# Twelve projections of an attention layer by seven products of half-size blocks in place of eight

## The chip, the cores and the metric

The kernel runs on one core of a Trainium2 chip. The metric is the device time of one execution in microseconds (us), the median of repeated runs. The core has a matrix engine (TensorE, "PE" in the profile; its weight loads are "PEld"), which multiplies into a memory of its own called PSUM (in banks; a tile of 128 x 512 float32 numbers fills one), and three engines that work on vectors: VectorE ("DVE"), ScalarE ("ACT") and GpSimd ("POOL"). SyncE ("SP") issues transfers. GpSimd is given operands in ordinary on-chip memory alone in this kernel; what lies in PSUM is taken out by VectorE or ScalarE. Engines run side by side and wait for each other by semaphores.

## The reference, cut to what matters

A batch of 4 images with 512 channels of 32 x 32 = 1024 tokens goes through four layers, each added to its input after a group normalisation. The change touches layer 2 alone, an attention with 8 heads of 64 channels:

```python
def _L2_conv_ref(x, Wq, bq, Wkv, bkv, Wp, bp):
    ...
    q = _conv1x1(x, Wq, bq)                  # 512 x 512 weight on 512 x 1024 values
    kv = _conv1x1(x, Wkv, bkv)
    k, v = jnp.split(kv, 2, axis=1)
    ...
    attn = jnp.einsum('bhct,bhcs->bhts', q, k) * SCALE
    attn = jax.nn.softmax(attn, axis=-1)
    out = jnp.einsum('bhts,bhcs->bhct', attn, v)
    ...
    out = _conv1x1(out, Wp, bp)
    return out

    # --- layer 2 (conv_preact) ---
    x = x + _L2_conv_ref(_gn(x), L2_conv_Wq, ...)
```

Per image that is four projections (q, k, v and the output p), each a product of a 512 x 512 weight and 512 x 1024 values, and between them the scores, the softmax and the weighted sum of v. Everything is in float32. Layer 0 is another attention, layer 1 a gate, layer 3 a search for the 8 nearest of 2048 stored items.

## The kernel before: layer 2

P is 128, NB 512, T 1024 (tokens), C 512, KC 4 (groups of 128 channels), TC 8 (groups of 128 tokens). A projection is 32 matmuls of 128 x 128 weights on 512 columns. Four at a time add up in one bank, and eight fill a tile of two banks, which one operation takes out. The tiles come from a pool of three ("sc"), so the next eight matmuls have another tile:

```python
def project(w, rhs, m, at, evacuate, name="proj"):
    ps = place(at, f"{name}_{m}")            # ps_s.tile([P, 2, NB], F32, tag="sc")
    for n in range(T // NB):
        for k in range(KC):
            pin(nc.tensor.matmul(                            # L197
                ps[:, n, :], w[:, k, m * P:(m + 1) * P], rhs(k, n),
                start=(k == 0), stop=(k == KC - 1)))
    evacuate(flat2(ps))
```

`project_tokens` (L209) does the same for v, with tokens as rows. q is taken out by DVE (L935, with bias and the factor SCALE), k by ACT (L942), v by DVE with its bias (L951). The attention of an image is cut into 16 units of four groups of keys; the scores of one unit stand beside the weighted sum of the unit before it:

```python
def scores2(b, u, before=None):
    ...
    nc.scalar.activation(e, scs[len(es)], AF.Exp)            # L967
    ...
    pin(nc.tensor.matmul(sc[:, r, :], I["k"][...], I["q"][...], ...))   # L973
    ...
    # the sum of the exponentials: pairs on GpSimd, pairs of pairs on VectorE
    nc.gpsimd.tensor_add(I["es", m, n], es[0], es[1])        # L987
    nc.gpsimd.tensor_add(two, es[i], es[i + 1])              # L991
    nc.vector.tensor_add(I["es", m, n], I["es", m, n], two)  # L992

def finish2(b):                                              # a head pair's end
    ...                                                      # rs: matmuls with ones, L1027
    nc.scalar.copy(ri, rsp)                                  # L1032
    nc.vector.reciprocal(ri, ri)                             # L1033
    nc.vector.tensor_mul(I["o"][...], pv, ri)                # L1034
    ...                                                      # two small transfers by GpSimd, L1037

def put_out2(b):                                             # output projection and residual
    def add_out(m, ps):
        for n in range(T // NB):
            xr = apool.tile([P, NB], F32, tag="xr", bufs=2, ...)
            nc.sync.dma_start(out=xr, in_=x1[b][:, m, n * NB:(n + 1) * NB])    # L1048
            nc.scalar.activation(xr, xr, AF.Identity, bias=I["tb"]..., scale=s1...)  # L1049
            nc.vector.tensor_add(xr, ps[:, n * NB:(n + 1) * NB], xr)           # L1051
            nc.sync.dma_start(out=x2[b][:, m, n * NB:(n + 1) * NB], in_=xr)    # L1052
            nc.vector.bn_stats(st[:, n, :], xr)                                # L1053
    for m in range(KC):
        project(I["Wp"], tokens(I["o"]), m, None, lambda ps: add_out(m, ps), ...)
```

The loop over the images, cut:

```python
for b in range(B):
    for s, u in enumerate(UNITS2):                  # 16 units
        if s == 5 and not last: load2(b + 1)        # Wq, Wk, Wv of the next image
        if s >= 1: scores2(b, u, UNITS2[s - 1])
        for _ in range(2):
            if s >= 3: next(behind, None)           # small steps of other layers
            if s >= 8: next(ahead, None)            # the next image's normalisation
    if not last:
        for m in range(KC): take_q2(b + 1, m)       # q of the next image
        img[b]["Wp"] = load_w("Wp", ...)
    apply2(b, UNITS2[-1])                           # the last unit's weighted sum
    if not last:
        for m in range(KC): take_k2(b + 1, m)       # k of the next image
    finish2(b)
    if not last:
        for i in range(TC // 2): take_v2(b + 1, i)  # v of the next image
        scores2(b + 1, UNITS2[0])                   # its first unit
    put_out2(b)                                     # p of this image
```

The sums and the last head pair's end thus fall into the time of q and of v; the last DVE and POOL operations of the attention are still under way when q begins. Image 0's q, k and v are made in layer 1's part, outside this loop.

Of the kernel before, what the change touches and what calls it, by code (L numbers as in the profile page):

```python
# [41 lines left out]
def fast_net(ctx: ExitStack, tc: tile.TileContext, a: dict, out: bass.AP, flag: bass.AP):  # L42
# [33 lines left out]
    bp2 = chan(a["bp"], "bp2")  # L76
    fcb = chan(a["fc_b"], "fcb")
# [818 lines left out]

    count = [0]
# [33 lines left out]
    def take_q2(b, m, at=None):  # L931
        I = img[b]
        if m == 0:
            I["q"] = big("q", f"q2_{b}")
        project(I["Wq"], tokens(I["xn"]), m, at, lambda ps: pin(nc.vector.tensor_scalar(  # L935
            I["q"][:, m, :], ps, bq2[:, m:m + 1], SCALE, ALU.add, ALU.mult)), f"q2_{b}")
# [8 lines left out]
    def take_v2(b, i, at=None):  # L945
        I = img[b]
        if i == 0:
# [3 lines left out]
            lambda ps: pin(nc.vector.tensor_add(  # L951
                I["v"][:, 2 * i:2 * i + 2, :], ps,
                bv2.rearrange("p c -> p () c").to_broadcast([P, 2, C]))), f"v2_{b}")

    def scores2(b, u, before=None):
# [8 lines left out]
        def exp2():  # L964
            e = places2[:, count[0] % 6]
            count[0] += 1
            nc.scalar.activation(e, scs[len(es)], AF.Exp)  # L967
# [17 lines left out]
        if t0 == 0:  # L985
            I["es", m, n] = sums2[:, (2 * m + n) % 2]
            nc.gpsimd.tensor_add(I["es", m, n], es[0], es[1])  # L987
            es = es[2:]
        for i in range(0, len(es), 2):
            two = pair_sum[:, (t0 + i) // 2 % 2]  # L990
            nc.gpsimd.tensor_add(two, es[i], es[i + 1])  # L991
            nc.vector.tensor_add(I["es", m, n], I["es", m, n], two)  # L992
# [45 lines left out]

    def put_out2(b):
        I = img[b]  # L1040
        s1 = l2[b][1]
        mv = small.tile([P, KC, 2], F32, tag="mv", name=f"mv_d{b}")

        def add_out(m, ps):
            st = small.tile([P, 2, 6], F32, tag="bnst", name=f"st_d{b}_{m}")
            for n in range(T // NB):
                xr = apool.tile([P, NB], F32, tag="xr", bufs=2, name=f"xr_c{b}_{m}_{n}")
                nc.sync.dma_start(out=xr, in_=x1[b][:, m, n * NB:(n + 1) * NB])  # L1048
                nc.scalar.activation(  # L1049
                    xr, xr, AF.Identity, bias=I["tb"][:, m:m + 1], scale=s1[:, m:m + 1])  # L1050
                nc.vector.tensor_add(xr, ps[:, n * NB:(n + 1) * NB], xr)  # L1051
                nc.sync.dma_start(out=x2[b][:, m, n * NB:(n + 1) * NB], in_=xr)  # L1052
                nc.vector.bn_stats(st[:, n, :], xr)  # L1053
# [1027 lines left out]
```

## Time and profile before

| what | value |
|---|---|
| median of 3 runs | 2745.2 us (2741.17 to 2746.28) |
| span of the profiled run | 2741.6 us |
| mean TensorE clock granted | 0.98 of full speed |
| layer 2 in the span | about 1375 to 2225 us |
| attention stages of image 0, 1, 2, 3 | 1375 to 1508, 1628 to 1746, 1865 to 1985, 2104 to 2225 us |
| projection stages between them | 1508 to 1628, 1746 to 1865, 1985 to 2104 us |

The span is the time from the first to the last instruction of one execution; it is read in windows, stage by stage, since each stage has a limit of its own. For each window the profile gives the busy time of each engine with the number of its instructions, and the clock that TensorE was granted. The rows of groups give, for a line of the kernel and an engine, what is written from what, the shape, how often, the busy time and the mean of one in ns, and then the idle time of the engine ahead of them with what ended it. A group with DVE as its engine that reads a tile written by PE takes a result out of PSUM. Three such rows of layer 2, which the steps below speak of:

```profile
L1032 ACT COPY ri_c<-rs_c 128x512 f32<-128x512 f32 x32 | 18.7, 585 | 49.9 <-PE rs_c L1027 49.9
L1051 DVE TENSOR_TENSOR xr_c<-p,xr_c 128x512 f32<-128x512 f32 x24 | 15.5, 687 | 42.3 <-PE p L197 38.2 <-ACT xr_c L1049 4.1
L650 DVE SCALAR_TENSOR_TENSOR xr<-mx,bproj,xr 128x512 f32<-128x512 f32 x6 | 4.5, 745 | 11.4 <-PE mx L197 8.9 <-DMA xr<-in_x 2.5
```

### The profile page before, as it was taken

Reading aid. Unit: us, or ns where it says so; the run is one execution under the profiler, and the core shown is the slowest. Engines: PE = TensorE matmul, PEld = TensorE weight load, DVE = VectorE, ACT = ScalarE, POOL = GpSimd, SP = SyncE. Lnnn points to the kernel's source line nnn. Section 1 sums busy time; section 2 is a strip of 40 time slices with the busy share of each in tenths; the row PEclk is TensorE's granted clock in tenths of the full one; section 3 lists DMA queues with packets and bytes.
Section 4 is the critical chain, followed back from the end, with each engine's and each line's share of the span. In section 5 each row is a group of like instructions: output and inputs, shape, how many; then the busy total and the mean of one; then the engine's idle time right before and its main releaser. Section 6 shows DMA issues by size and latency. Waiting matters only on the chain.

```text
span 2741.6 us, 46996 instructions
## 1 busy us (share of the span) xinstructions
PE 2593.0 (95%) x18286; PEld 1180.3 (43%) x18286; DVE 1522.8 (56%) x2386; ACT 1007.6 (37%) x1149; POOL 1266.2 (46%) x1955
## 2 busy tenths in 40 slices
PE   8988999989989898989999999999999999999995
PEld 3443544545445444545433433343343334444442
DVE  5487337871588526873235224513623537788886
ACT  0565336551565426552154025214502622121210
POOL 2266325552455514653067017305702735666664
PEclk9999999999999999999999999999999999999997
DMA  2577438880687627785310030021002016767665
GB/s 78 128 206 204 128 93 219 218 216 28 172 216 202 164 69 193 205 207 199 116 32 1 31 123 1 16 77 62 1 31 92 1 48 189 220 186 216 185 183 148
DMA packets 159321, 349.82 MB, mean 128 GB/s; under 512 B 32361, under 2 KB 65129, under 8 KB 155378
## 3 DMA queue, kind: packets, MB, share of 16 engines
q1 hardware_dynamic: 86304, 167.04, 21.2%
q0 software_dynamic: 51200, 142.93, 19.3%
q10 hardware_dynamic: 21586, 36.76, 4.6%
q8 instruction: 147, 2.41, 0.4%
q14 instruction: 84, 0.69, 0.1%
HBM read 178.57 MB, written 33.69 MB: 77 GB/s over the span
## 4 chain that ended last, share of the span: by engine, by line
PE 82%; DMA 7%; ACT 4%; DVE 2%; issue 1%; POOL 1%; SPq 1%; ACTq 0%; POOLq 0%; DVEq 0%
PE at L1094 16%; PE sc_c L973 7%; PE pv_c L1006 7%; PE sc L451 7%; PE mx L197 7%; PE pv L511 6%; PE pt L410 4%; DMA s<-ss 4%; PE p L197 4%; PE sc L197 4%; PE v L209 3%; PE k L197 3%; PE q L197 3%; PE pt L684 3%; ACT ss L457 2%; PE mx L471 2%
## 5 line engine op out<-in xcount | busy, mean ns | idle before, releaser
L484 DVE STREAM_TRANSPOSE eT<-e 128x1024 f32<-128x1024 f32 x256 | 317.6, 1242 | 273.9 <-ACT e L478 272.0
L464 POOL DMA_DIRECT2D s<-ss x512 | 259.8, 515 | 384.4 <-ACT ss L457 299.6
L1111 POOL DMA_INDIRECT got<-in_mem,ix x256 | 280.2, 1095 | 208.3 <-DVE tmx L1117 92.3
L457 ACT COPY ss<-sc 128x1024 f32<-128x1024 f32 x256 | 258.9, 1011 | 264.4 <-PE sc L451 212.7
L967 ACT ACTIVATE eT<-sc_c 128x1024 f32<-128x1024 f32 x256 | 247.9, 1021 | 275.3 <-PE sc_c L973 213.3
L500 DVE BATCH_NORM_STATS2 st<-e 128x6 f32<-128x256 f32 x1024 | 341.6, 406 | 0.0
L451 PE MATMUL sc<-k,q 64*32 64x512 f32 x4096 | 287.1, 617 | 22.5 <-ACT ss L457 17.6
L991 POOL TENSOR_TENSOR e<-eT 128x1024 f32<-128x1024 f32 x96 | 231.3, 2412 | 164.7 <-ACT eT L967 133.2
L478 ACT ACTIVATE e<-mx 128x1024 f32<-128x1024 f32 x256 | 262.5, 1029 | 65.5 <-PE mx L471 28.0
L992 DVE TENSOR_TENSOR eT<-eT,e 128x1024 f32<-128x1024 f32 x96 | 132.8, 1384 | 274.0 <-POOL e L991 274.0
L511 PE MATMUL pv<-eT,v 128*64 128x128 f32 x4096 | 256.5, 279 | 0.0
L973 PE MATMUL sc_c<-q,k 64*128 64x512 f32 x1024 | 243.2, 614 | 11.3 <-ACT eT L967 9.0
L511 PEld LDWEIGHTS pv<-eT,v 128*64 128x64 f32 x4096 | 226.1, 139 | 63.9 <-issue 62.3
L1006 PE MATMUL pv_c<-eT,v 128*64 128x512 f32 x1024 | 234.4, 600 | 0.0
L471 PE MATMUL mx<-s,wmix 32*32 32x512 f32 x4096 | 159.6, 625 | 45.0 <-DMA s<-ss 44.9
L1135 DVE SCALAR_TENSOR_TENSOR acc<-got,et,acc 128x512 f32<-128x512 f32 x224 | 168.4, 752 | 8.0
L1033 DVE RECIPROCAL ri_c<-ri_c 128x512 f32<-128x512 f32 x32 | 107.0, 3345 | 96.1 <-ACT ri_c L1032 96.1
L973 PEld LDWEIGHTS sc_c<-q,k 64*128 64x128 f32 x1024 | 94.9, 189 | 144.0 <-issue 74.7
L1099 ACT COPY att<-at 128x1024 f32<-128x1024 f32 x64 | 64.8, 1012 | 217.8 <-PE at L1094 217.6
L987 POOL TENSOR_TENSOR eT<-eT 128x1024 f32<-128x1024 f32 x32 | 76.0, 2374 | 147.0 <-ACT eT L967 146.8
L587 POOL TENSOR_TENSOR o<-pv,rb 64x256 f32<-64x256 f32 x128 | 111.1, 868 | 67.1 <-ACT pv L574 60.2
L1006 PEld LDWEIGHTS pv_c<-eT,v 128*64 128x64 f32 x1024 | 70.9, 138 | 155.2 <-issue 154.6
(317 smaller groups left out, 3325.5 us busy)
## 6 DMA issues: line engine op xcount, KB each, us to landing
s<-ss SPq DMA_DIRECT2D x512, 128.0 KB
s<-ss POOLq DMA_DIRECT2D x512, 128.0 KB, 4.4
rb<-r POOLq DMA_DIRECT2D x64, 128.0 KB, 5.9
o<-o SPq DMA_DIRECT2D x32, 256.0 KB
xr<-in_x ACTq DMA_DIRECT2D x32, 256.0 KB
x<-xr SPq DMA_DIRECT2D x32, 256.0 KB
xr_c<-x SPq DMA_DIRECT2D x32, 256.0 KB
x<-xr_c SPq DMA_DIRECT2D x32, 256.0 KB
```

What stands on the lines that cost most here:

```text
L197: pin(nc.tensor.matmul(ps[:, n, :], w[:, k, m * P:(m + 1) * P], rhs(k, n), start=(k == 0), stop=(k == KC - 1),))
L451: pin(nc.tensor.matmul(sc[m * NS:(m + 1) * NS, r, :], q[r * HD:(r + 1) * HD, m, s * NS:(s + 1) * NS], k_[r * HD:(r + 1) * HD, m, n * NB:(n ...
L457: pin(nc.scalar.copy(ss[:, :, n * NB:(n + 1) * NB], sc))
L464: pin(relays[r].dma_start(out=s2[r * KC + m::NH], in_=ss[m * NS:(m + 1) * NS, r, :]))
L478: pin(nc.scalar.activation(e[:, half].rearrange("p r qq k -> p (r qq k)"), flat2(pairs[f"mx{half}"]), AF.Exp))
L484: pin(nc.vector.transpose(eT[:, j % 2].rearrange("p b (qq i r) x -> p i r qq b x", qq=2, i=4)[:, i, 2 * half:2 * half + 2], e[:, half].rea ...
L500: pin(nc.vector.bn_stats(st[:, i, 2 * half + r, qq, :], e[:, half, r, qq, :]))
L511: pin(nc.tensor.matmul(pv[r * HD:(r + 1) * HD, gp, :], I["v"][:, t, g * HD:(g + 1) * HD], eT[:, j % 2, t, :, 4 * g:4 * g + 4], start=(t == ...
L973: pin(nc.tensor.matmul(sc[:, r, :], I["k"][r * HD:(r + 1) * HD, m, t * P:(t + 1) * P], I["q"][r * HD:(r + 1) * HD, m, n * NB:(n + 1) * NB] ...
L1006: pin(nc.tensor.matmul(pv[r * HD:(r + 1) * HD, :], I["v"][:, t, h * HD:(h + 1) * HD], e[:, r, :], start=(t == 0), stop=(t == TC - 1),))
L1094: pin(nc.tensor.matmul(sc[:, n * NB:(n + 1) * NB], xn3[b][:, k, tt * P:(tt + 1) * P], memT[k][:, i0:i0 + NB], start=(k == 0), stop=(k == K ...
L1111: pin(nc.gpsimd.indirect_dma_start(out=got[:, i, :], out_offset=None, in_=a["mem"], in_offset=bass.IndirectOffsetOnAxis(ap=ix[:, i:i + 1], ...
```

## The change

A product of two matrices, each cut into 2 x 2 blocks, takes eight products of blocks. Strassen's scheme in Winograd's form takes seven, at the price of sums of blocks: four sums on the weight's side, four on the values' side, and seven on the products' side. The change does this for twelve of layer 2's sixteen projections: q, k and v of images 1 to 3 and p of images 0 to 2. The sums of weight blocks are made by GpSimd, those of value blocks by VectorE, both ahead of the projection; those of products by VectorE as the products come. It comes in two halves a projection, each with two tiles of the pool of three. The whole list of what it alters:

- `seven_w`, `seven_x`: the sums ahead of use. `seven`: the order of the seven products and what takes them out.
- The factor SCALE moves from q to the exponential, since bias and factor would not fit q's new evacuation.
- The bias of v is left out of v and carried: the softmax's weights add to one, so bv goes through to the output as Wp times bv, a column that `carry_bias` makes once and that is added to the output's bias.
- The eight pieces of the image that p's output is added to are loaded ahead of p, six of them into a region that the stored items of layer 3 held until now; those items are loaded in the last image.
- The sums of the last unit's exponentials are written behind q (`later`), the next image's normalisation begins two units earlier, and the statistics of a piece are taken two pieces later.

The core of the diff, with cuts:

```diff
+    def seven_w(w, nm):
+        ...
+        nc.gpsimd.tensor_add(s1, block(1, 0), block(1, 1))
+        nc.gpsimd.tensor_sub(s2_, s1, block(0, 0))
+        nc.gpsimd.tensor_sub(s4, block(0, 1), s2_)
+        nc.gpsimd.tensor_sub(block(1, 0), block(0, 0), block(1, 0))
+        return None, block(0, 0), block(0, 1), s4, block(1, 1), s1, s2_, block(1, 0)
+    def seven_x(x, places):
+        ...
+        nc.vector.tensor_sub(t1, block(0, 1), block(0, 0))
+        nc.vector.tensor_sub(block(0, 1), block(1, 1), block(0, 1))
+        nc.vector.tensor_sub(t2, block(1, 1), t1)
+        nc.vector.tensor_sub(t4, block(1, 0), t2)
+        return None, block(0, 0), block(1, 0), block(1, 1), t4, t1, t2, block(0, 1)
+    def seven(product, put, nm):
+        ag = ps_s.tile([P, 2, NB], F32, tag="sc", name=f"ag_{nm}")
+        de = ps_s.tile([P, 2, NB], F32, tag="sc", name=f"de_{nm}")
+        product(1, ag[:, 0], True)
+        u2 = apool.tile([P, NB], F32, tag="o1", name=f"u2_{nm}")
+        nc.scalar.copy(u2, ag[:, 0])
+        product(6, ag[:, 1], True)
+        nc.vector.tensor_add(u2, u2, ag[:, 1])
+        product(7, de[:, 1], True)
+        u3 = apool.tile([P, NB], F32, tag="o2", name=f"u3_{nm}")
+        nc.vector.tensor_add(u3, u2, de[:, 1])
+        product(5, de[:, 0], True)
+        put(1, 1, u3, de[:, 0])
+        product(2, ag[:, 0], False)      # adds to p1, still in the bank
+        put(0, 0, None, ag[:, 0])
+        product(4, de[:, 1], False)      # adds to p7
+        put(1, 0, u2, de[:, 1])
+        product(3, de[:, 0], False)      # adds to p5
+        put(0, 1, u2, de[:, 0])
+    def project7(A, X, out, bias, nm):   # q and k; project7_tokens is the same for v
+        for m in range(2):
+            def put(i, j, u, ps):
+                ...
+                if u is None:
+                    nc.scalar.activation(o, ps, AF.Identity, bias=bias[:, c:c + 1])
+                else:
+                    nc.vector.scalar_tensor_tensor(o, u, bias[:, c:c + 1], ps, ALU.add, ALU.add)
+            seven(seven_by_channels(A, X, m), put, f"{nm}_{m}")
...
-            nc.scalar.activation(e, scs[len(es)], AF.Exp)
+            nc.scalar.activation(e, scs[len(es)], AF.Exp, scale=SCALE)
...
+    def carry_bias(b):
+        for m in range(KC):
+            for k in range(KC):
+                pin(nc.tensor.matmul(
+                    ps[:, m:m + 1], img[b]["Wp"][:, k, m * P:(m + 1) * P], bv2[:, k:k + 1], ...))
...
+        def add_block(m, n, u, ps):      # p: one piece of the output
+            xr = I.pop(("xr2", m, n))
+            if u is None:
+                nc.vector.tensor_add(xr, ps, xr)
+            else:
+                y = apool.tile([P, NB], F32, tag="rb", bufs=2, ...)
+                nc.vector.tensor_add(y, u, ps)
+                nc.gpsimd.tensor_add(xr, xr, y)
+            store(m, n, xr)
+            ...                          # ACT scales the piece three further on
...
+            if s in (8, 9) and not last:
+                img[b + 1]["A", key] = seven_w(img[b + 1][key], ...)      # Wq, Wk
...
+            if s == 12 and not last:
+                run_out(ahead)
+                img[b + 1]["X"] = seven_x(img[b + 1]["xn"], thirds(halves2))
         if not last:
-            for m in range(KC):
-                take_q2(b + 1, m)
-            img[b]["Wp"] = load_w("Wp", f"Wp2_{b}")
+            take7(b + 1, "Wq")
+            for add_up in later:
+                add_up()
+            J["A", "Wv"] = seven_w(J["Wv"], f"Wv{b + 1}")
+            I["Wp"] = load_w("Wp", f"Wp2_{b}")
         apply2(b, UNITS2[-1])
         if not last:
-            for m in range(KC):
-                take_k2(b + 1, m)
+            take7(b + 1, "Wk")
+            if b == 0:
+                carry_bias(b)
+            I["A", "Wp"] = seven_w(I["Wp"], f"Wp{b}")
         finish2(b)
...
+            I["O"] = seven_x(I["o"], [...])
+            take7(b + 1, "Wv")
+            nc.gpsimd.tensor_add(I["tb"], I["tb"], cb)
+            for at in range(len(ORDER2)):
+                load_piece2(b, at)
             scores2(b + 1, UNITS2[0])
         put_out2(b)
```

The last image keeps the plain output projection, and image 0 its plain q, k and v.

## The prediction

> **What bounds the kernel now.** I read the page's first part, then the waits of TensorE in layer 2, which the change is confined to (1375 to 2225 us of the span).
>
> ```profile
> PE 2593.0 (95%) x18286; PEld 1180.3 (43%) x18286; DVE 1522.8 (56%) x2386; ACT 1007.6 (37%) x1149; POOL 1266.2 (46%) x1955
> ```
>
> ```profile
> PE sc_c L973 <- ACT eT L967: 9.0, 4, 2.8
> PE amp L841 <- POOL amp L833: 4.3, 1, 4.3
> ```
>
> In 850 us TensorE waits 13.3 us (columns: total, times, longest). Next, the windows by stage, one attention stage and one projection stage, then the whole layer (columns: PE, weight loads, DVE, ACT, POOL busy, granted clock, DMA share, GB/s).
>
> ```profile
> 1508.00:1628.00 120.00, 120.00 (x298) 51.38 (x296) 32.67 (x32) 13.27 (x16) 11.26 (x8) 1.00 0.20 70
> 1628.00:1746.00 118.00, 115.44 (x517) 40.73 (x514) 61.41 (x42) 64.44 (x74) 84.19 (x57) 1.00 0.07 19
> ...
> 1375.00:2225.00 850.00, 836.66 (x3007) 324.25 (x3004) 338.62 (x257) 306.24 (x351) 377.07 (x284) 0.99 0.11 37
> ```
>
> The projection stage has TensorE at 120 of 120 us, with DVE at 33 and ACT at 13. So TensorE alone sets the time here, and each of its microseconds is one of the kernel's, saved or lost. The chain of waits gives the price of a projection, and the groups its count.
>
> ```profile
> 1508.68 27.66 PE q L197 x64
> 1536.34 3.58 PE pv_c L1006 x16
> 1539.93 27.66 PE k L197 x64
> ...
> 1568.60 27.66 PE v L209 x64
> 1596.27 3.63 PE sc_c L973 x16
> 1599.90 27.68 PE p L197 x64
> ```
>
> ```profile
> L197 PE MATMUL q<-xn_c,Wq 128*128 128x512 f32 x192 | 83.2, 594 | 0.0
> ...
> L684 PE MATMUL pt<-of,w_p 128*128 128x256 f32 x384 | 96.0, 393 | 0.0
> ```
>
> A projection is 32 matmuls of the program; each shows as two records, so 64. 27.66 / 64 = 0.432 us from record to record, though one record lasts 594 ns: 0.16 us of it is the tail that the next record covers. A 256-wide record lasts 393 ns; a run of eight in layer 0 takes 1.99 us from first start to last end, so (1.99 - 0.38) / 7 = 0.230 us each.
>
> **What the Trainium skill says.** "Perfetto Trace Analysis", section Matmuls: independent groups should rotate through different PSUM banks, so that emptying one lies beside the next group's matmuls. The kernel before does, and shows no wait for an evacuation in its projections. "PSUM — Partial Sum Buffer", section "PSUM bank collisions raise a hardware error": guard by bank and quadrant; different banks run clean. That matters because the changed program, as built, guards by tile, and its tiles are two banks each: stricter than the chip asks. No run here shows a collision. "TensorE: Matmul & The Clock Gate", "What's actually happening": an idle window of some 3.4 us halves TensorE's clock. The trace agrees: after its one wait of 4.3 us (ending 1449.28) the clock is
>
> ```profile
> 1446.00:1450.00 4.00, 0.72 (x4) 0.72 (x4) 0.21 (x1) 0.00 (x0) 2.23 (x5) 0.79 0.01 1
> 1450.00:1454.00 4.00, 4.00 (x12) 2.16 (x13) 0.14 (x1) 1.35 (x3) 4.00 (x3) 0.50 0.00 0
> ```
>
> and sixteen score records take 5.86 us there in place of the 3.63 above: 2.2 us lost. "VectorE: DVE Perf Modes", section on the TRN2 errata: an fp32 tensor_tensor of 512 elements takes 691 ns by its formula; here 687 (xr_c L1051, reading PSUM).
>
> **The change, part by part.**
>
> *Removed: matmuls.* A projection of seven half-size products is 28 matmuls of 512 columns, 56 records. For the nine q, k and p: 9 x 8 x 0.432 = -31.1 us. The three v take 112 records of 256 columns: 112 x 0.230 = 25.8 against 27.66, so -5.7 us. Together -36.8.
>
> *Added: waits of TensorE inside every product group.* This is the step I rest on. I read the built program's semaphore waits for one half of a projection (p1, p6, p7, p5, p2, p4, p3 in its order). A half keeps its sums in two tiles, ag and de, of two banks each. The program orders accesses by tile, so p6, which writes ag's second bank, waits for ACT's copy of ag's first; p5 waits for DVE's u3, which reads de's other bank; p3 waits for DVE's output of p4. Each of these sits directly behind the product it depends on, with nothing between for TensorE to do. The waits of p4 (on an evacuation that p2 covers) are free. The trace has one such handover, in layer 1's last projection:
>
> ```profile
> 1299.94 14.18 PE mx L197 x33
> ...
> 1314.14 1.12 ACT k L942
> 1315.26 0.04 issue
> 1315.30 4.99 PE mx L209 x11
> ```
>
> So a handover costs the tail (0.16), the engine's operation, some 0.04 us on either side, and 0.1 us because the first record behind it lasts 697 ns, not 594. With ACT's 128x512 copy from PSUM (585 ns, L1032): 0.16 + 0.04 + 0.585 + 0.04 + 0.105 = 0.93. With DVE's 0.69 us addition: 1.03, rounded up to 1.08 since DVE often has another operation in hand. For q and k the third is a scalar_tensor_tensor of 0.745 (xr<-mx L650): 1.15. A half costs 0.93 + 1.08 + 1.1 = 3.1 us; 24 halves: **+75 us**.
>
> *Moved: DVE at the start of q.* Before, DVE is in arrears when q begins at 1508.7:
>
> ```profile
> 1511.21 3.35 DVE L992 TENSOR_TENSOR eT<-eT,e 128x1024 f32<-128x1024 f32 x1 [2.53 <-POOL e L991]
> 1514.49 3.34 DVE L1033 RECIPROCAL ri_c<-ri_c 128x512 f32<-128x512 f32 x1
> 1517.75 1.16 DVE L992 TENSOR_TENSOR eT<-eT,e 128x1024 f32<-128x1024 f32 x1
> 1518.83 0.67 DVE L1034 TENSOR_TENSOR eT<-pv_c,ri_c 128x512 f32<-128x512 f32 x1
> ```
>
> It is free 10.7 us into q. There q's first DVE operation was needed late; now u2 and u3 queue behind all this, and p5 waits for u3. The change means to put these sums off, but in the built order they stand ahead of u2 as before. p5 could start at 7.15 us (three products at 1.73, plus 0.93 and 1.03) and starts at about 10.7 + 1.5 = 12.2: +5 us, thrice, **+15**. That idle stretch of 6 us exceeds the 4.3 that halved the clock above: 2 us more each, **+6**.
>
> *Smaller.* The carried bias is 16 matmuls of one column, 32 records of 0.16 to 0.19 us, once: +5.5. At v the same reciprocal, with the four new differences of o behind it on DVE (4 x 1.23), delays u3 by 1.2: +3.6. In p, DVE and POOL hand pieces to each other and POOL may be held by the next weight's sums: +5 by judgement. Sums inside the attention stages (four DVE operations of 1.23, four POOL operations of about 1.2 per weight, on a POOL at 84 of 118 us): +4, of 0 to 12. The pieces loaded ahead remove the store-then-load chain that idled TensorE 2.56 us behind p (1640.11), but their scaling stands ahead of the scores' exponentials on ACT: +2 net.
>
> Sum: -36.8 + 75 + 15 + 6 + 5.5 + 3.6 + 5 + 4 + 2 = +79, from 2745.2 to 2824. The small terms were taken at their full size, so I take 2820.
>
> **The rivals.** *As intended* (no exposed waits): TensorE saves 36.8 and pays 5.5 for the bias: about 2715. For it: TensorE is the bound, and the other engines have room in the projection stages. Against: the waits stand in the built program, and no other matmul lies between. *Waits by bank only* (p6, p5 and p3 free, but DVE late at q, and POOL): -36.8 + 5.5 + 15 + 15 gives about 2740. For it: the skill's rule asks for no more; against: the program does. *A deeper backlog* (the clock falls at many short gaps, DVE and POOL chase each other in p): every half loses 1 to 2 us more, 2850 to 2870. Against: TensorE stays near 80% busy in the halves, and the one wait of 1.08 us in the trace costs nothing behind it.
>
> **Range and chances.** The 75 is 72 waits of known make; an error of 0.2 us in each is 14 us. The q start may be 5 to 30, the rest 5 to 35. So 2796 to 2845. A 2% gain needs 2690, below even the intended case: 0.01. Within 2% (up to 2800): 0.15. Slower: 0.84.
>
> **What would show it.** In the changed profile, the waits of TensorE would list ag and de behind ACT's u2 copy, DVE's u3 and DVE's outputs, about 24 times each (the third split over q and k, v, p), the first near 0.7 us of idle time each. A k projection would span 24.2 + 6.2 = 30.4 us where it spans 27.66, and q about 36, with a gap of some 6 us before its fourth product. Matmul records of the nine would be 56 for 64. TensorE's share of the span would fall below 95%. I am wrong if these waits are absent or much shorter than 0.7 us (the tail or the handover misjudged), if DVE is free at q's start, or if the attention stages of about 120 us stretch by more than the 4 us allowed for all of them.

## The result and the profile after

The changed kernel takes 2859.4 us (median of 4 runs, 2847.5 to 2863.0) where the kernel before takes 2745.7: a ratio of 1.0408, interval 1.0378 to 1.0437. The prediction, 2820 with a range of 2796 to 2845, had the direction and its main step, and was 39 us short. The profiled runs have spans of 2855.3 and 2741.6 us; the 113.7 us between them are what the following accounts for.

The page's first part: TensorE is a little longer busy than before, and its share has fallen by four points.

```profile
PE 2599.2 (91%) x18390; PEld 1202.4 (42%) x18390; DVE 1617.0 (57%) x2488; ACT 1020.7 (36%) x1180; POOL 1350.4 (47%) x2025
```

The waits of TensorE (columns: total, times, longest), the lines of layer 2. The whole list before had two in this layer, 13.3 us. L959 and L983 are the products, L940 is ACT's copy u2, L945 VectorE's sum u3, L1113 VectorE's addition of the exponentials, and L1153 the row sums of a head pair (`rs`), which need it.

```profile
PE de_q L959 <- DVE u_q L945: 24.4, 6, 7.5
...
PE de_p L959 <- DVE u_p L945: 16.6, 6, 7.0
...
PE rs_c L1153 <- DVE eT L1113: 10.6, 4, 6.7
...
PE de_v L983 <- DVE u_v L945: 8.3, 6, 2.0
PE de_p L959 <- DVE y_c L1226: 7.7, 6, 1.4
...
PE de_k L959 <- DVE k L973: 5.0, 6, 0.8
...
PE de_k L959 <- DVE u_k L945: 4.7, 6, 0.8
...
PE ag_k L959 <- ACT u_k L940: 4.1, 6, 0.7
```

k has the three waits of the prediction in each of its six halves, at 0.7 to 0.8 us of idle time. q, v and p have the same, and in some halves much longer ones. The chain of waits through half of one k (start, duration, what) shows the pattern; each piece of TensorE is one product of four records.

```profile
1555.64 1.93 PE ag_k L959 x4
1557.57 0.02 issue
1557.59 0.59 ACT u_k L940
1558.19 0.04 issue
1558.23 1.98 PE ag_k L959 x4
1560.21 1.73 PE de_k L959 x4
1561.94 0.02 issue
1561.97 0.70 DVE u_k L945
...
1562.71 1.98 PE de_k L959 x4
```

The second product does not start at 1557.4, one product after the first, but after ACT's copy; the fourth after VectorE's addition.

The stages by the timeline, from first record to last end, in us. Three values are those of the three images that make the projections; the attention stages are from the end of p to the next q; the last column is image 3's attention with the first block of layer 3.

| kernel | q | k | v | p | attention, image 1 and 2 | image 3 |
|---|---|---|---|---|---|---|
| before | 27.7 27.7 27.7 | 27.7 27.7 27.7 | 27.7 27.7 27.7 | 27.7 27.7 27.7 | 118.3 120.0 | 134.8 |
| after | 39.1 39.7 39.4 | 30.5 30.5 30.5 | 35.3 33.5 33.5 | 40.0 39.0 31.6 | 126.9 123.0 | 136.2 |

Beside these there are 5.0 us more between k and v of image 0 (the carried bias), and layer 2 begins 5.1 us later. The latter can't be put down to the change: over the profiles of all kernels told of below, layer 2's first score record stands between 1370.5 and 1382.1 us, and kernels with the seven products stand on both sides of the kernel before (1372.8): 1372.1 with the last sums later, 1379.6 with four tiles. What moves it is not shown.

### The profile page after: what moved, and what is told of

Read it like the earlier page. It is cut to its first block, busy times and chain, and to the rows that moved or that the text cites. A ratio compares the mean times of both kernels' runs of the same rounds, so it can differ in the third digit from the quotient of the medians.

```text
span 2855.3 us, 47539 instructions
## 1 busy us (share of the span) xinstructions
PE 2599.2 (91%) x18390; PEld 1202.4 (42%) x18390; DVE 1617.0 (57%) x2488; ACT 1020.7 (36%) x1180; POOL 1350.4 (47%) x2025
## 4 chain that ended last, share of the span: by engine, by line
PE 67%; DMA 7%; DVE 7%; issue 6%; POOL 6%; ACT 5%; SPq 1%; ACTq 0%; POOLq 0%; DVEq 0%
PE at L1286 15%; PE sc L452 7%; PE mx L198 7%; PE pv L512 5%; DMA s<-ss 4%; PE pt L411 4%; PE pv_c L1132 4%; PE sc_c L1091 4%; PE sc L198 4%; ACT ss L458 3%; PE pt L685 3%; POOL e L1112 2%; PE de_q L959 2%; PE de_k L959 2%; PE mx L472 1%
## 5 line engine op out<-in xcount | busy, mean ns | idle before, releaser
L1113 DVE TENSOR_TENSOR eT<-eT,e 128x1024 f32<-128x1024 f32 x96 | 149.6, 1559 | 268.2 <-POOL e L1112 268.1
L1112 POOL TENSOR_TENSOR e<-eT 128x1024 f32<-128x1024 f32 x96 | 232.2, 2425 | 65.8 <-DVE eT L1113 32.5
L1091 PE MATMUL sc_c<-q,k 64*128 64x512 f32 x1024 | 245.2, 617 | 10.8 <-ACT eT L1085 8.3
L452 PEld LDWEIGHTS sc<-k,q 64*32 64x32 f32 x4096 | 47.6, 106 | 188.8 <-ACT ss L458 138.9
L1286 PE MATMUL at<-memT,xn_d 128*128 128x512 f32 x256 | 120.6, 593 | 0.0
```

The lines of the kernel that those rows point to most:

```text
L452: pin(nc.tensor.matmul(sc[m * NS:(m + 1) * NS, r, :], q[r * HD:(r + 1) * HD, m, s * NS:(s + 1) * NS], k_[r * HD:(r + 1) * HD, m, n * NB:(n ...
L1091: pin(nc.tensor.matmul(sc[:, r, :], I["k"][r * HD:(r + 1) * HD, m, t * P:(t + 1) * P], I["q"][r * HD:(r + 1) * HD, m, n * NB:(n + 1) * NB] ...
L1112: nc.gpsimd.tensor_add(two, rest[i], rest[i + 1])
L1286: pin(nc.tensor.matmul(sc[:, n * NB:(n + 1) * NB], xn3[b][:, k, tt * P:(tt + 1) * P], memT[k][:, i0:i0 + NB], start=(k == 0), stop=(k == K ...
```

## The experiments

Each edit is against the changed kernel unless another is named. Ratios are to the kernel before on the same chip, whose median is 2744.9 to 2745.9 us in all of them, so that "less" is counted from the changed kernel's 2859.4. Stage times are from one profiled run each.

**Four tiles.** Each of the four running sums of a half gets a tile of its own, so that no product writes a tile that another engine is reading.

```diff
-        ag = ps_s.tile([P, 2, NB], F32, tag="sc", name=f"ag_{nm}")
-        de = ps_s.tile([P, 2, NB], F32, tag="sc", name=f"de_{nm}")
+        a_ = ps_s.tile([P, 2, NB], F32, tag="sc", name=f"a_{nm}")[:, 0]
+        g_ = ps_s.tile([P, 2, NB], F32, tag="sc", name=f"g_{nm}")[:, 0]
+        d_ = ps_s.tile([P, 2, NB], F32, tag="sc", name=f"d_{nm}")[:, 0]
+        e_ = ps_m.tile([P, NB], F32, tag="mm", name=f"e_{nm}")
```

> The changed kernel (2859.4 us) with each of the four running sums of a product group in a PSUM tile of its own (three of the pool of three, one of the other pool), so that no product waits for an operation that reads a neighbouring bank. My theory (waits by tile behind p1, p7 and p4 are the largest loss): a k projection falls from 30.5 us to about 24.3, v from 33.5 to about 26.5, q from 39.4 to about 29.5 and p from 40 to about 30, as the late VectorE now holds up only the sixth product; in all about -95 us, 2765 (2750 to 2790). Rival (the engines that take the products out are too slow or contended, and the waits only change their place): 2840 or more.

Measured: 2774.0 us, 1.0097 (1.0072 to 1.0123); 85 us less. The chain through the same half of k now has TensorE alone:

```profile
1552.37 1.91 PE a_k L961 x4
1554.28 1.72 PE g_k L961 x4
1556.00 1.72 PE d_k L961 x4
1557.71 1.72 PE e_k L961 x4
```

Fourteen such pieces stand end to end, and k takes 24.3 us for 30.5: 6.2 us for the six handovers of a projection, 1.03 us each. v takes 24.4, the last p 24.3. q is still at 33 to 34: its e tile comes from the pool in which a head pair's sum waits for the late VectorE (waits of up to 7.1 us for the multiplication that frees it), which the expectation had not seen. The rival falls: in k, the engines that take the products out keep up with TensorE once it need not wait for them. The 85 us are more than the handovers: v and p fell by 28 and 24 us over three images, where their handovers are worth 18 and 21, since the lateness of VectorE went in part too. Image 3's stage is 6 us longer than before; no run here explains that.

**The side parts alone.** Plain projections, no sums of blocks; bias carried, pieces ahead, factor in the exponential.

```diff
-            take7(b + 1, "Wq")
+            for m in range(KC):
+                take_q2(b + 1, m)
...
-                seven(
-                    seven_by_channels(I["A", "Wp"], I["O"], m),
-                    lambda i, j, u, ps: add_block(2 * i + m, j, u, ps), f"p2_{b}_{m}")
+                project(I["Wp"], tokens(I["o"]), m, None, ...)   # add_block on its halves
```

> The changed kernel with plain projections and without any sums of blocks; the carried bias, the factor in the exponential, the pieces loaded ahead, the earlier normalisation and the later stored items stay. My theory (these side parts cost the carried bias, about 5 us, and win back at most 3): 2747 to 2755. Rival (the side parts cause the loss): 2800 or more.

Measured: 2750.6 us, 1.0015 (1.0002 to 1.0028). The side parts cost about what the carried bias does (5 us); the loss lies in the products and their sums.

**The last sums later.** The sums of the last unit's exponentials are pinned behind q on both engines.

```diff
-                nc.gpsimd.tensor_add(two, rest[i], rest[i + 1])
-                nc.vector.tensor_add(I["es", m, n], I["es", m, n], two)
+                hold(nc.gpsimd.tensor_add(two, rest[i], rest[i + 1]))
+                hold(nc.vector.tensor_add(I["es", m, n], I["es", m, n], two))
```

`hold`, and `pin` below, keeps an instruction behind what its engine has already in the program; other instructions may move ahead in the built order.

> The changed kernel with the last unit's sums of exponentials held behind q on GpSimd and VectorE, which the change meant and the built order did not do. My theory (VectorE's arrears hold the fourth product of q): the wait of 7.5 us falls to 1 to 2 in each of three images, and the halved clock behind it goes: -22 us, about 2837 (2830 to 2845). Rival (the sums only move their delay, to k or to v): within 8 us of 2859.

Measured: 2816.2 us, 1.0258 (1.0228 to 1.0288); 43 less. q falls to 30.5 us in all three images, which is k's price: the six waits for u3 in q come to 4.7 us, from 24.4. That is 27 us for the 22 expected: the waits give 19.7, the slower records behind them the rest. The other 16 are outside q: 9 in the two attention stages (119.7 and 121.1 us), which I had not expected, and 6 ahead of layer 2, where runs differ anyway.

**The weight sums at their place.** In the built order GpSimd makes the sums of the next image's Wq as soon as that weight has landed, ahead of the first unit's sums; here they stay where the program has them, in the units 8 and 9.

```diff
-        nc.gpsimd.tensor_add(s1, block(1, 0), block(1, 1))
+        pin(nc.gpsimd.tensor_add(s1, block(1, 0), block(1, 1)))
```

> The changed kernel with the sums of weight blocks held at their place in the program on GpSimd, so that those of the next image's Wq no longer stand ahead of the first unit's sums while p begins. My theory (they hold VectorE and with it the fourth product of p in images 0 and 1): that wait falls from 7 us to about 2 and p from 40 to about 32 us, twice: -16 us, about 2843 (2836 to 2850). Rival (it is the DMA of the pieces or of Wq that holds p): within 5 us of 2859.

Measured: 2868.0 us, 1.0440 (1.0403 to 1.0476): slower, a miss. The part that was to fall fell: p is at 31.6 us in all three images. But the attention stages of images 1 and 2 are now 134.2 and 133.1 us, and q of image 0 begins at 1528.9 in place of 1512.9, 2.3 us of which lie ahead of layer 2. The sums are some five us of GpSimd for a weight, and they cost more in the middle of the attention than in p.

**No weight sums.** All four sums of every weight are left out; the products take plain blocks in their place, so the values are not those of a projection.

```diff
-        nc.gpsimd.tensor_add(s1, block(1, 0), block(1, 1))
-        ...
-        return None, block(0, 0), block(0, 1), s4, block(1, 1), s1, s2_, block(1, 0)
+        return None, block(0, 0), block(0, 1), block(0, 0), block(1, 1), block(0, 1), block(1, 1), block(1, 0)
```

> The changed kernel without the sums of weight blocks on GpSimd (leaves them out: the products take plain blocks in their place). My theory after the run with these sums held at their place (2868: p fell to 31.6 us, but the attention stages grew by 33 us over three images): they cost wherever GpSimd has the exponentials' sums to do. Expected: p of images 0 and 1 from 40 and 39 to 31.6 us, attention stages within 3 us of the changed kernel's, 2841 (2834 to 2848). Rival (p is held by DMA, or the growth of the attention stages has another cause): within 5 us of 2859.

Measured: 2825.7 us, 1.0293 (1.0257 to 1.0329); 34 less, nearly twice what was expected. p is at 31.5, as expected. The surplus is in the attention stages, 118.4 and 119.4 us against 126.9 and 123.0, and in v (32.5 in the first two for 35.3 and 33.5); 5 us lie ahead of layer 2. q stays at 38.3 to 39.9.

**No value sums** of the next image (its four VectorE operations), left out in the same way.

```diff
-                img[b + 1]["X"] = seven_x(img[b + 1]["xn"], thirds(halves2))
+                img[b + 1]["X"] = (None, q_[0], q_[2], q_[3], q_[2], q_[1], q_[3], q_[1])   # plain blocks
```

> The changed kernel without the sums of value blocks of the next image on VectorE (leaves them out for q, k and v: the products take plain blocks in their place). My theory (these four operations, behind the normalisation, hold up the reciprocal and with it TensorE by 6.7 us in image 1 and halve its clock): the attention stages fall by 8 us in image 1 and by 1 to 3 in image 2; 2848 (2842 to 2855). Rival (the normalisation alone, begun two units earlier, does it): within 4 us of 2859.

Measured: 2822.3 us, 1.0281 (1.0235 to 1.0327); 37 less, where 11 were expected. The attention stages are at 119.6 and 118.6, and q at 36.5, 30.5, 30.5: without these four operations VectorE is in time for q in two images of three. That is the clue to a state of the attention stage which I had not seen, though the kernel before has it too. The timeline of the changed kernel, VectorE and then GpSimd, over one round of two units (columns: start, duration, instruction, count, idle time before and its releaser):

```profile
1772.24 3.35 DVE L1159 RECIPROCAL ri_c<-ri_c 128x512 f32<-128x512 f32 x1
...
1781.59 1.23 DVE L1113 TENSOR_TENSOR eT<-eT,e 128x1024 f32<-128x1024 f32 x1 [4.33 <-POOL e L1112]
1785.35 3.36 DVE L1113 TENSOR_TENSOR eT<-eT,e 128x1024 f32<-128x1024 f32 x1 [2.53 <-POOL e L1112]
1788.63 3.34 DVE L1159 RECIPROCAL ri_c<-ri_c 128x512 f32<-128x512 f32 x1
```

```profile
1776.90 2.36 POOL L1108 TENSOR_TENSOR eT<-eT 128x1024 f32<-128x1024 f32 x1
1779.21 2.35 POOL L1112 TENSOR_TENSOR e<-eT 128x1024 f32<-128x1024 f32 x1
1782.96 4.66 POOL L1112 TENSOR_TENSOR e<-eT 128x1024 f32<-128x1024 f32 x2 [1.40 <-DVE eT L1113]
```

VectorE and GpSimd wait for each other in turn, and the round is 1788.63 - 1772.24 = 16.4 us. TensorE needs 15.3 us for two units: its row sums in the same kernel, earlier in the stage, stand that far apart (1739.50, 1754.80). So an engine pair that has fallen behind in this state doesn't catch up in it, and here TensorE is caught: its next row sums come 22.0 and then 16.8 us later (1776.81, 1793.60).

```profile
1754.80 1.08 PE L1153 MATMUL rs_c<-eT,ones 128*64 128x512 f32 x4
...
1776.81 1.97 PE L1153 MATMUL rs_c<-eT,ones 128*64 128x512 f32 x4 [6.65 <-DVE eT L1113]
```

In the kernel before, image 1 ends in the same round of 16.4 us, but the stage is over before TensorE is reached: its last row sums there are still 15.3 us apart (1726.13, 1741.42).

```profile
1733.91 3.34 DVE L1033 RECIPROCAL ri_c<-ri_c 128x512 f32<-128x512 f32 x1
...
1750.32 3.34 DVE L1033 RECIPROCAL ri_c<-ri_c 128x512 f32<-128x512 f32 x1
```

One addition in it takes 3.36 us where the same one beside it takes 1.23: GpSimd's second addition runs to 1782.96 + 4.66 = 1787.62, and VectorE's, issued at 1785.35, ends 1.1 us after that. In the kernel without value sums no addition is so long in images 1 and 2 once they are past the normalisation, and the round there follows TensorE:

```profile
1763.97 1.23 DVE L1113 TENSOR_TENSOR eT<-eT,e 128x1024 f32<-128x1024 f32 x1 [2.53 <-POOL e L1112]
1765.11 3.35 DVE L1159 RECIPROCAL ri_c<-ri_c 128x512 f32<-128x512 f32 x1
...
1780.24 3.35 DVE L1159 RECIPROCAL ri_c<-ri_c 128x512 f32<-128x512 f32 x1
```

15.1 us from reciprocal to reciprocal. The Trainium skill has a reason for the long addition ("SBUF — State Buffer", section "Who interferes with whom"): a VectorE instruction with two inputs in SBUF (on-chip memory outside PSUM) contends with a GpSimd instruction that reads SBUF. The trace agrees here with 3.36 against 1.23 us; VectorE's additions in the projections, with one input in PSUM, are at 0.63 to 0.69 us throughout. The trace also shows that it matters which of the two starts first. In layer 2 of the changed kernel, 17 of these additions take 2.27 to 3.38 us, and each of them began 0.07 us or more behind a GpSimd operation that was still running; 12 others overlap with a GpSimd operation that began after them, and take 1.16 to 1.23 us.

**No sums at all.** Neither weights nor values (xn and o), left out as above.

> The changed kernel without any sums of blocks ahead of the products, neither of weights (all four) nor of values (xn and o): it leaves them out, and the products take plain blocks. The seven products a group, their two tiles and all that takes them out stay. My theory (without the sums neither VectorE nor GpSimd is in arrears, and only the waits by tile are left: 30.5 us for q and k, about 32.5 for v, 31.5 for p, carried bias 5, attention stages as before): 2745 + 3 x (125 - 111) + 5 = 2792 (2783 to 2802). Rival (the arrears of VectorE at q are the kernel before's own, and stay without the sums): 2810 or more.

Measured: 2805.8 us, 1.0213 (1.0177 to 1.0248), between the two expectations and just outside mine. k 30.5, v 30.5 in two images, p 31.5, attention stages 118.1 and 118.4: as the theory has it. But q is 36.5, 30.5 and 37.5. In two images of three VectorE is late all the same, as it was in the kernel before, where nothing waited for it. So the sums of blocks are not the only cause of the arrears, and the rival has a part. In the profile the two late images are those in which the round of 16.4 us runs on into q; in image 1, at 30.5, the last round is 15.1 us.

**Tiles and order together**, the first constructive attempt: four tiles, the last sums behind q, and the first unit's sums of the next image between the halves of p.

```diff
-            scores2(b + 1, UNITS2[0])
-        put_out2(b)
+            scores2(b + 1, UNITS2[0], None, between)
+        put_out2(b, between if not last else [])
...
+                if m == 0:
+                    for add_up in between:
+                        add_up()
```

> The changed kernel with four tiles for the running sums (as in the run with four tiles, 2774), the last unit's sums held behind q (as in the run with later sums, 2816), and the first unit's sums of the next image held between the halves of p. My theory (the three losses add up: waits by tile, VectorE late at q, VectorE late at p): q, k, v and p all at 24.3 to 25.5 us, so the twelve save about 38 us against 27.7 each, less 5 for the carried bias: 2716 (2705 to 2730), below the kernel before. Rival (with the waits gone, VectorE and GpSimd become the bound of the projections): 2745 or more.

Measured: 2742.3 us, 0.9993 (0.9976 to 1.0010): level with the kernel before and close to the rival's figure, but not for its reason, since q, k and v are at 24.3 to 25.0, which saves 29 us over three images. p is at 26.9, 26.9 and 28.6 and saves nothing to speak of. The rest is lost again: the attention stages are 3.5 and 3.2 us longer than in the kernel before, image 3's 5.6, the bias costs 4.5, and the scores ahead of p 5.3.

**q, k and v alone.** p plain; the weight sums of Wq and Wk on VectorE in units 4 and 5, their loads in unit 0; four tiles and the last sums behind q as before.

```diff
-            if s in (8, 9) and not last:
-                key = ("Wq", "Wk")[s - 8]
-                img[b + 1]["A", key] = seven_w(img[b + 1][key], f"{key}{b + 1}")
+            if s in (4, 5) and not last:
+                key = ("Wq", "Wk")[s - 4]
+                img[b + 1]["A", key] = seven_w(img[b + 1][key], f"{key}{b + 1}", nc.vector)
```

> Seven products for q, k and v alone (p plain, with its pieces loaded ahead), in four tiles, with the last unit's sums behind q, and with the weight sums of Wq and Wk on VectorE in the first units of an image, those of Wv on GpSimd beside k. My theory (what the four-tile version with its order mended, 2742, gave back lies in p, 9 us over three images against a saving of 10, and in GpSimd's sums in the attention stages, about 11): q and k at 24.3 us, v at 24.4, together -30; carried bias +5; scores ahead of p +3; attention stages +2 each: 2728 (2720 to 2738), about 0.6% below the kernel before. Rival (the attention stages grow by the same 3 to 5 us whichever engine makes the sums): 2742 or more.

Measured: 2752.7 us, 1.0032 (1.0021 to 1.0043): the rival's side. The projections are as expected (v of image 0 is at 26.5), and the attention stages take 129.6 and 128.4 us, with TensorE waiting 17.1 us in all (6.9 at the longest) for VectorE's sum of exponentials ahead of the row sums.

**Normalisation on ScalarE**, in the version just told.

```diff
-            pin(nc.vector.tensor_scalar(
-                xn[:, k, :], xn[:, k, :], sa[:, k:k + 1], ta[:, k:k + 1],
-                ALU.mult, ALU.add,
-            ))
+            pin(nc.scalar.activation(
+                xn[:, k, :], xn[:, k, :], AF.Identity, bias=ta[:, k:k + 1], scale=sa[:, k:k + 1]))
```

> As the version with seven products for q, k and v alone, and the next image's normalisation on ScalarE in place of VectorE. My theory (it is VectorE's work late in the attention stage, normalisation and value sums together, that lengthens it; ScalarE is busy 64 of 118 us there): 2 to 6 us less than that version. Rival (ScalarE's exponentials are what TensorE waits for in that stage, and four operations of 1.1 us among them cost as much): equal to it or up to 12 us more.

Measured: 2743.2 us, 0.9992 (0.9981 to 1.0004); 9.6 less, more than the 2 to 6 of the theory. The attention stages are at 126.4 and 126.6, and the same wait is 9.7 us.

**The sums beside the projections**, from there on. The weight sums of Wq and Wk move into the projection stage of the image before, on VectorE, with their loads behind q and k.

```diff
             take7(b + 1, "Wv")
+            if b + 2 < B:
+                img[b + 2]["A", "Wq"] = seven_w(img[b + 2]["Wq"], f"Wq{b + 2}", nc.vector)
...
             for m in (2, 0, 3, 1):
+                if m == 3 and b + 2 < B:
+                    img[b + 2]["A", "Wk"] = seven_w(img[b + 2]["Wk"], f"Wk{b + 2}", nc.vector)
                 project(
```

> As the version with seven products for q, k and v alone and the normalisation on ScalarE (2743), but the weight sums of Wq and Wk are made by VectorE in the projection stage of the image before (at the end of v and within p), where it is busy 33 of 120 us, and their loads come behind q and k. My theory (the attention stage has no room for more work on VectorE or GpSimd, the projection stage has): the attention stages of images 1 and 2 fall from 126.5 us by 4 to 8 each, p and v grow by at most 1; 2731 (2724 to 2738), below the kernel before. Rival (the value sums and the carried bias alone keep the stage long): 2740 or more.

Measured: 2742.0 us, 0.9990 (0.9976 to 1.0003). The point at issue came out as the theory has it: the attention stages fall to 120.2 and 118.5 us, level with the kernel before, and v and p do not grow. The total did not follow, for two faults of my edit in image 0: there the sums stood in the attention stage (141 us), and Wp was loaded behind Wq, so that the carried bias waited:

```profile
PE amp L837 <- POOL amp L817: 5.1, 1, 5.1
...
PE cb L1173 <- DMA Wp<-in_Wp: 3.2, 1, 3.2
```

**Image 0 mended**, against the version just told. Both faults undone. GpSimd's sums are no longer pinned, and in the built order those of image 1's Wq and Wk run at 1293 and 1321 us, ahead of layer 2, as in the changed kernel (1296 and 1324); in the version just told they ran at 1408 and 1414.

```diff
-        pin(eng.tensor_add(s1, block(1, 0), block(1, 1)))
+        first = eng.tensor_add(s1, block(1, 0), block(1, 1))
+        if eng is nc.vector:
+            pin(first)
...
-            if s == 4 and b == 0:
-                for key in ("Wq", "Wk"):
-                    img[1]["A", key] = seven_w(img[1][key], f"{key}1", nc.gpsimd)
+            if s in (8, 9) and b == 0:
+                key = ("Wq", "Wk")[s - 8]
+                img[1]["A", key] = seven_w(img[1][key], f"{key}1", nc.gpsimd)
...
+            I["Wp"] = load_w("Wp", f"Wp2_{b}")
             if b + 2 < B:
                 img[b + 2]["Wq"] = load_w("Wq", f"Wq2_{b + 2}")
-            I["Wp"] = load_w("Wp", f"Wp2_{b}")
```

> As the version with the sums beside the projections (2742), with two faults of it mended: image 1's weight sums of Wq and Wk are again made on GpSimd where the changed kernel makes them, instead of within image 0's attention stage (141 us there, 135 in the changed kernel), and Wp is loaded ahead of the next Wq (k to v in image 0 took 12 us, 5 of them the carried bias). My theory: -6 and -6, 2730 (2724 to 2737), about 0.5% below the kernel before. Rival (image 0's stage is long for the value sums, not for the weight sums): 2738 or more.

Measured: 2723.3 us, 0.9925 (0.9913 to 0.9938): 22 us below the kernel before, a little more than the theory had, and the only version that beats it clearly. By the stages, q, k and v save 28.9 us, and the carried bias and the scores ahead of p take 7.1 back, which leaves 21.8. Image 0's attention stage is 5.5 us shorter than before, but so it is without any seven products (6.4 with the side parts alone), and other small differences are against it. Not run: the kernel before with the normalisation on ScalarE alone. TensorE's waits in layer 2 are back at about what the kernel before had:

```profile
PE sc_c L1093 <- ACT eT L1087: 7.5, 5, 2.7
PE amp L842 <- POOL amp L834: 4.0, 1, 4.0
PE sc_c L1093 <- DVE xr L651: 2.7, 1, 2.7
PE rs_c L1156 <- DVE eT L1116: 0.7, 1, 0.7
```

| kernel | q | k | v | p | attention, image 1 and 2 | image 3 |
|---|---|---|---|---|---|---|
| four tiles | 34.2 33.8 33.2 | 24.3 24.3 24.3 | 25.2 24.4 24.4 | 31.6 30.6 24.3 | 123.4 124.7 | 140.8 |
| last sums later | 30.5 30.5 30.5 | 30.5 30.5 30.5 | 35.2 33.5 33.5 | 39.9 38.5 31.6 | 119.7 121.1 | 136.2 |
| weight sums at their place | 39.2 38.1 39.8 | 30.5 30.6 30.6 | 35.3 31.8 33.5 | 31.6 31.6 31.6 | 134.2 133.1 | 136.2 |
| no weight sums | 38.3 38.7 39.8 | 30.5 30.5 30.5 | 32.5 32.5 34.1 | 31.5 31.5 31.5 | 118.4 119.4 | 135.7 |
| no value sums | 36.5 30.5 30.5 | 30.5 30.5 30.5 | 35.3 33.5 33.5 | 37.7 37.5 31.6 | 119.6 118.6 | 137.8 |
| no sums at all | 36.5 30.5 37.5 | 30.5 30.5 30.5 | 32.3 30.5 30.5 | 31.5 31.5 31.5 | 118.1 118.4 | 137.3 |
| image 0 mended | 24.9 24.3 24.6 | 24.3 24.3 24.3 | 25.1 24.4 24.4 | 27.7 27.7 27.7 | 120.0 118.8 | 134.4 |

## Why the prediction was right in kind and too small

The step that failed is the paragraph "Smaller" of the prediction. It put the lateness of VectorE at v and at p, and the sums within the attention stages with the pieces, at 3.6, 5 and 6 us; they measured 10.8, 16.1 and 14. These three are 26 of the 34 us between the two sums below; VectorE late at q is 6 more. The prediction's own sign came true in this: the attention stages of images 1 and 2 stretched by 11.5 us, where it allowed 4 for all. Term by term, over three images, from the table (24.3 and 24.4 are the bare products of the four-tile run; 30.5 and 31.5 the products with their waits alone, from the run with no sums at all):

| step | predicted | measured | how measured |
|---|---|---|---|
| matmuls saved | -36.8 | -40.7 | 9 x (27.73 - 24.30) + 3 x (27.73 - 24.44) |
| waits by tile | +75 | +77 | 3 x (6.2 for q + 6.2 for k + 6.1 for v + 7.2 for p) |
| VectorE late at q, with the clock | +21 | +26.7 | 118.2 - 3 x 30.5 |
| late at v | +3.6 | +10.8 | 102.3 - 3 x 30.5 |
| late at p | +5 | +16.1 | 110.6 - 3 x 31.5 |
| sums in the attention stages, pieces | +6 | +14 | 8.6 + 2.9 + 1.4, and 1.2 ahead of p |
| carried bias | +5.5 | +5.0 | gap between k and v of image 0 |
| ahead of the first q | 0 | +4 | q of image 0 begins 4.3 later |
| sum | +79 | +113 | the spans: +113.7 |

**Right: the waits by tile.** This was the step I rested on. 77 us for 75, with 1.03 us a handover in k, and the run without them was 85 us faster. The intended case is refuted by it, and so is the case of waits by bank only.

**Right in kind, short in size: VectorE late at q.** The fourth product was to start 12.2 us into q and starts 13.9 us into it, since the arrears at q's start were 1.7 us larger than before: VectorE comes to u2 12.4 us into q, where it was free after 10.7. The gap is the 7.5 us of the list, and the clock behind it halved as predicted: the windows of the changed kernel at the end of the gap (column 6 is the clock) are

```profile
1522.00:1526.00 4.00, 0.00 (x0) 0.00 (x0) 3.93 (x4) 0.00 (x0) 1.00 (x2) 0.73 0.01 1
1526.00:1530.00 4.00, 3.22 (x4) 1.51 (x5) 0.69 (x1) 0.00 (x0) 0.00 (x0) 0.50 0.00 0
```

and four records take 3.78 us there for 1.98.

**Wrong: "+5 by judgement" for p.** I had named the cause there (GpSimd held by the next weight's sums) and did not work it out, though the built order shows the place. GpSimd and VectorE at the start of p, image 0:

```profile
1632.26 1.26 POOL L914 TENSOR_TENSOR s_Wq<-Wq 128x512 f32<-128x512 f32 x1 [34.88 <-DMA Wq<-in_Wq]
...
1636.04 2.34 POOL L1108 TENSOR_TENSOR eT<-eT 128x1024 f32<-128x1024 f32 x1
1638.34 1.26 POOL L916 TENSOR_TENSOR s_Wq<-Wq,s_Wq 128x512 f32<-128x512 f32 x1
1639.56 2.34 POOL L1112 TENSOR_TENSOR e<-eT 128x1024 f32<-128x1024 f32 x1
```

```profile
1641.93 1.22 DVE L1113 TENSOR_TENSOR eT<-eT,e 128x1024 f32<-128x1024 f32 x1 [13.94 <-POOL e L1112]
...
1643.86 0.69 DVE L945 TENSOR_TENSOR u_p<-u_p,de_p 128x512 f32<-128x512 f32 x1
```

VectorE stands 13.9 us before one addition of the softmax, with u2 and u3 of p behind it in its queue, and TensorE waits 7.0 us for u3, then works at half clock: 8.4 and 7.4 us in images 0 and 1. Image 2, with no next image, has 31.6. The runs with the weight sums moved or left out, p at 31.6 and 31.5 in all images, settle this.

**Wrong: "four DVE operations of 1.23".** In the attention stage these operations do not all have the duration of a lone one. The groups of layer 2, first the old additions in the kernel before, then the changed kernel:

```profile
L992 DVE TENSOR_TENSOR eT<-eT,e 128x1024 f32<-128x1024 f32 x96 | 132.8, 1384 | 274.0 <-POOL e L991 274.0
...
L1113 DVE TENSOR_TENSOR eT<-eT,e 128x1024 f32<-128x1024 f32 x96 | 149.6, 1559 | 268.2 <-POOL e L1112 268.1
...
L927 DVE TENSOR_TENSOR eT<-xn_c 128x1024 f32<-128x1024 f32 x3 | 8.2, 2723 | 0.1
L928 DVE TENSOR_TENSOR xn_c<-xn_c 128x1024 f32<-128x1024 f32 x3 | 7.8, 2588 | 0.1
```

The means of 2.7 and 2.6 us mix two kinds: of the twelve value sums of three images eight take 1.2 us, and four, which overlap with GpSimd, take 3.3 (three of them) and 5.7. The old additions are 1.56 us on average where they were 1.38. What I took for room (VectorE at 61 of 118 us, GpSimd at 84) was none: the two wait for each other through the softmax's sums, in a round of 16.4 us when late against TensorE's 15.3. Leaving out the weight sums or the value sums each takes 12 us off the attention stages of images 1 and 2, and leaving out both takes 13. So in these stages the two are not separate terms: leaving out either brings them back to 118 to 120 us. (On the whole kernel the three runs gain 34, 37 and 54 us, with intervals of some 10 us each, too wide to show this by themselves.) Beside this, the value sums are paid for at q (97.5 us in all without them, 118.2 with) and the weight sums at p (94.4 for 110.6).

**v: the delay right, what follows it left out.** The prediction had u3 later by 1.2 us for the differences of o, and TensorE's wait there is 2.0 us in place of 0.8. But the clock falls behind this wait too, and the next two products of image 1 take 2.7 and 2.9 us for 2.0 and 1.9; image 0 is 1.7 us longer still, its first product taking 3.7 us at half clock behind the one-column matmuls of the carried bias. So a wait of 2.0 us was enough here, less than the 4.3 and the 3.4 us that the prediction spoke of:

```profile
1880.00:1884.00 4.00, 2.85 (x9) 2.40 (x10) 2.31 (x4) 0.00 (x0) 0.00 (x0) 0.78 0.00 0
```

The 256-wide records, estimated at 0.230 us, came out at 24.44 / 112 = 0.218, which hid part of it.

**Rounding, and the rivals.** I worked out +79 and wrote 2820, in the belief that the small terms were full-sized. They were all too small. The deeper backlog's 2850 to 2870 held the result, and part of its reason: VectorE and GpSimd did wait for each other, at p and still more in the attention stages. Its other reason did not hold in general: k, with three short gaps in every half, keeps its 30.5 us at full clock (1.00 from 1556 to 1572 us). The terms of the rival by bank add up to 2744 and not 2740, which changes nothing.

What stays open: which operation starts the round of 16.4 us. It is in the kernel before, so the seven products do not create it, and q was late in just those images in which it ran on into q: all three of the changed kernel and of the one without weight sums, image 0 without value sums, images 0 and 2 without any. The run with the normalisation on ScalarE lowers the wait for VectorE (17.1 to 9.7 us), but this was not tried without the sums.

## What to carry to other kernels

A scheme that saves multiplications turns each product's result into something that the next steps wait for: give every running sum that another engine reads between two products a PSUM tile of its own, so that the waits of the built program follow the data and not the tile (85 us here). Before sums are placed on an engine that looks half idle, look for the round in which it and another engine wait for each other, and compare its length with that of TensorE's stage; then put the sums where that round does not run (the projection stages: 120.2 and 118.5 us of attention in place of 126.4 and 126.6). The scheme paid here only where its sums were free: 0.9925 for q, k and v, and nothing for p in the two orders tried without the waits by tile.

## What the runs showed of the hardware that was not expected

- A VectorE addition of two SBUF operands took 3.36 us behind a GpSimd addition that had begun 0.1 us earlier, and 1.23 us alone or where GpSimd's began later; in the long case it ended 1.1 us after GpSimd's. With one operand in PSUM, additions of 512 columns took 0.63 to 0.69 us in all places.
- A handover from TensorE to another engine and back left TensorE idle for 0.09 us more than the operation, with ACT (0.59 us copy, idle 0.68) as with VectorE (0.69 us addition, idle 0.78). The whole price was about 0.35 us above the operation (1.03 - 0.68 on average); the rest is the tail of the last record and the longer first record behind.
- Records of 256 columns have a pitch of 0.218 us in a long run (24.44 / 112), half of the 0.434 of 512 columns (24.30 / 56): no loss for the narrower form.
- TensorE's clock fell behind a wait of 2.0 us in v (0.78 of full speed from 1880 to 1884 us, the wait ending at 1881.15), and not behind the waits of 0.7 to 0.8 us in k.
